# Scores of the last layer from high and low float32r halves instead of fp32 operands

## The chip, the cores and the metric

The kernel is one program on one core of a Trainium2 chip. The metric is device time in microseconds (us) of one execution, from launch to end. Three executions of the kernel before gave 3190.16, 3192.45 and 3198.47 us; their median, 3192.45 us, is what "before" means below. All durations inside the kernel come from one further execution that was profiled.

A core has a matrix engine (PE, with a separate row PEld for loading its stationary operand), three engines for elementwise work (DVE, ACT, POOL), and a queue, SP, which issues nearly all copies between DRAM and the on-chip memory here. A copy is moved by up to 16 DMA engines. Each engine runs its own instructions in order and waits for the others through semaphores. On-chip memory has 128 partitions; a matrix product contracts over partitions, and its result goes to PSUM, a separate memory that DVE and ACT read.

## The reference

The reference is a network of four layers on an input `x` of shape (4, 1024, 128). Each layer computes `x = x + s * silu(g)` with `s` from a mixing part and `g` from a feed-forward part, both on the normalized `x`. The change concerns the mixing part of the last layer, an attention with 16 heads of 8 numbers and a score that depends on distance:

```python
qx = split_head(x @ Wq.T)
kx = split_head(x @ Wk.T)
vx = split_head(x @ Wv.T)
ns = jnp.arange(n) + (MAXLEN - n)
ex = rel_embed[ns].reshape(n, NH, HD).transpose(1, 0, 2)
srel = srel_skew(jnp.einsum('bhnd,hmd->bhnm', qx, ex))
inv_dim = 1.0 / np.sqrt(d / NH)
qk = (jnp.einsum('bhnd,bhmd->bhnm', qx, kx) + srel) * inv_dim
mask = 1000000000.0 * jnp.triu(jnp.ones((n, n), dtype=x.dtype), 1)
atten = jax.nn.softmax(qk - mask, axis=-1)
out = jnp.einsum('bhnm,bhmd->bhnd', atten, vx).transpose(0, 2, 1, 3).reshape(b, n, d)
return out @ Wp.T + bp
```

`rel_embed`, the table of distance rows, has 256 rows while `n` is 1024, so most distances share one row; the kernel subtracts that row's vector from the others, and only a band of some four blocks of 128 columns beside the diagonal needs the distance term.

## The kernel before, in words

Layers 0 to 2 run first and end at about 2140 us of the profiled span. While layer 2 ends, `prepare3` (L1676) turns the weights of layer 3, and `begin_first` (L1864) makes the normalized input, the queries, the keys and the values of the first of the four batches and stores them in DRAM as `first["qk"]`, `first["vd"]` and `first["xnT"]`.

Layer 3 is `layer3` (L1725). Its work is cut into 16 groups: four batches, each with four sets `i` of four heads. A group has eight units, one for each block `t` of 128 query rows, taken in the order `ORDER3 = (7, 0, 6, 1, 5, 2, 4, 3)`, so that a long unit and a short one alternate. A unit with block `t` has (t+1) * 128 key columns, worked in tiles of at most 512; the units with t > 3 have two tiles, so a group has 12 tiles and the layer 192.

A head's 8 query numbers lie in partitions 32j to 32j+7 of a tile `q`, its keys in the same partitions of `k`, for j = 0 to 3; the other 24 of the 32 partitions of a head hold zeros, which `memset` (L1745) writes once. There are two pairs of `q` and `k`, used in turn by the groups. For each group:

- `project3` (L1968) loads `q` and `k` of the next group: four SP copies of 8 rows by 4096 bytes for `q`, and later four for `k` (L1975). The main loop asks for `q` at the first unit of a group (L1851) and for `k` at the third (L1854).
- `relative3` (L1992) multiplies 128 queries of two heads with the turned distance rows `W["emb"]` (L2004, tile `pr`), ACT copies the result to `r` (L2006), and SP stores `r` in a DRAM tile `flat` in four copies (L2009, L2010). It runs seven half-steps ahead of the unit that uses it.
- `shear3` (L2013) reads `flat` back with a row step one float short, which shifts every row by its distance (tile `rel`, L2025, L2027, L2031), and POOL masks and fills it with `select` (L2035). It runs three units ahead. The short units share one `rel` buffer, the long ones two.
- `scores3` (L2048) makes the scores: for one tile, four products, one a head, in the four 32-partition strips of PE (L2068, tile `score`, four times 512 floats of each partition of PSUM, one buffer). DVE adds `rel`, scales and keeps the minimum of the row (`neg`, L2076 and L2083, whose minimum is `low`), and ACT takes the exponent with a row sum (L2090).
- DVE transposes the weights in blocks of 32 (`wT`, L1797), and `weigh3` (L2096) multiplies them with the values on PE (L2104, tile `po`, 10240 instructions); `finish3` divides by the sums.

Beside a batch's groups run, in small steps, `ffn3` (L1942), the feed-forward part of that batch with its products `pgu` and `po` (L1953, L1963), and `begin3` (L1903), which makes queries, keys and values of the next batch and stores them as `seq["qk"]` (L1927). Most temporaries of these two, and `r`, take their place in turn from one pool of three buffers (tag `temp`).

The main loop (L1829 to L1859) writes out the order of all this for every engine. On PE, therefore, the scores of the next tile stand in one line with `pr`, `pgu` and both `po`. Every fp32 product is two instructions of PE and two weight loads in the profile: 192 tiles of four heads are 768 products of scores and 1536 instructions.

Of the kernel before, what the change touches and what calls it, by code (L numbers as in the profile page):

```python
# [10 lines left out]
F32 = mybir.dt.float32  # L11
BF16 = mybir.dt.bfloat16
I32 = mybir.dt.int32
AF = mybir.ActivationFunctionType
ALU = mybir.AluOpType
# [14 lines left out]
def _constants():  # L30
# [19 lines left out]
    parts.append(("sel16", (row // 16) == np.arange(8)[None, :]))  # L50

    parts.append(("rep8", np.where(row < 8, (col % 8) == row, 0.0)))

# [1613 lines left out]
def spread(a):  # L1667

    return a.rearrange("p (i j r) -> p i j r", j=4, r=32)[:, :, :, 0:8]
# [6 lines left out]
def prepare3(k, w, W, ps):  # L1676
# [20 lines left out]
    nc.gpsimd.tensor_copy(W["bpw"], W["bp"])  # L1697
    W["emb"] = new("emb", [P, 4, 256])
    with k.tc.tile_pool(name="pad3", bufs=1) as rp:
        pad = rp.tile([P, 2, 512], F32, tag="pad", name="pad")  # L1700
        nc.vector.memset(pad, 0.0)
        for c in range(2):
            for i in range(4):
                nc.gpsimd.tensor_copy(spread(pad[:, c, :])[:, i], heads_of(W["rel"][:, c, :])[:, i])
        for i in range(4):
            k.transpose_tiles(ps, "tr", [pad[:, c, i * P : (i + 1) * P] for c in (0, 1)], W["emb"][:, i, :])
            yield

        e0 = rp.tile([P, 4], F32, tag="e0", name="e0")
        nc.vector.tensor_copy(e0, W["emb"][:, :, 0])  # L1710
        for i in range(4):
            nc.vector.tensor_scalar(W["emb"][:, i, :], W["emb"][:, i, :], e0[:, i : i + 1], None, op0=ALU.subtract)
        nc.vector.tensor_scalar(W["emb"][:, :, 0], e0, -1.0, None, op0=ALU.mult)
# [11 lines left out]
def layer3(k, W, x3, out, eps5, ps, first):  # L1725
# [12 lines left out]
    with ExitStack() as st:  # L1738
# [123 lines left out]


def begin_first(k, W, pool, ps, x, eps5, first):  # L1864

# [8 lines left out]
    for n, name in enumerate(("WqT", "WkT")):  # L1874
        qk = pool.tile([P, T], F32, tag=("ret", "au")[n], name="qk")
        for half in range(2):
# [26 lines left out]
def begin3(k, W, p1, p2, temp, ps, dram, x3, b, eps5, seq):  # L1903
# [63 lines left out]

def project3(k, p2, pairs, seq, i, group):  # L1968

    nc = k.nc  # L1970
    q, kk = pairs
# [192 lines left out]
def tile_kernel(ctx: ExitStack, tc: tile.TileContext, I, out):  # L2164
# [11 lines left out]

    first = {name: store.tile(shape, F32, tag=name, name=name) for name, shape in (("qk", [2, P, T]), ("vd", [T, D]), ("xnT", [P, T]))}
    whole = ExitStack()
# [53 lines left out]
```

## Time and profile before

| What | Value |
|---|---|
| median of three executions | 3192.45 us |
| the profiled execution | 3191.88 us |
| its span from the first to the last instruction | 3190.2 us |
| layer 3 within the span | about 2144 to 3182 us |
| PE busy, whole span | 2246.5 us (70%) |
| DVE busy, whole span | 2302.6 us (72%) |
| ACT busy, whole span | 1494.7 us (47%) |
| POOL busy, whole span | 1155.6 us (36%) |
| mean granted clock of PE | 0.764 of full speed |
| score products, L2068 | 276.5 us in 1536 instructions |
| products with distance rows, L2004 | 227.5 us in 1024 instructions |

Busy time counts an instruction that executes; waiting, branching and the issuing of copies do not count. The instructions of PE are pipelined and overlap, so a mean duration is not the time between two starts. The number after a group's busy time in the profile is the mean of one instruction; behind the bar stands how long the engine sat idle just before that group's instructions and what ended the idle time. "issue" means that no releaser was found. The profile gives one line per group of instructions, by line of the kernel and by tile names `out<-in`.

### The profile page before, as it was taken

What the parts mean: (1) busy time and instruction counts of PE and PEld (TensorE: products, weight loads), DVE (VectorE), ACT (ScalarE), POOL (GpSimd) and SP (SyncE); (2) the same over time, 40 slices, a digit from 0 to 9 for tenths busy, and PEclk for the clock granted to TensorE, in tenths of its full rate; (3) what the DMA queues carried; (4) which work ended last, traced back from release to release, by engine and by line L of the source; (5) the groups of instructions that cost most, each with busy time, mean ns of one, the idle gap of its engine ahead of it and who ended that gap; (6) DMA issues with size and microseconds to landing.
All of it is one profiled execution on the core that took longest, in us unless ns stands there. A gap on an engine that the chain in (4) does not pass through costs nothing. (4 is left out here: it accounts for less than half of the span.)

```text
span 3190.2 us, 50621 instructions
## 1 busy us (share of the span) xinstructions
PE 2246.5 (70%) x18321; PEld 1278.9 (40%) x18321; DVE 2302.6 (72%) x5540; ACT 1494.7 (47%) x3256; POOL 1155.6 (36%) x1086
## 2 busy tenths in 40 slices
PE   5787778577787776894443674367877877878875
PEld 2555556232333332561110222244544544545553
DVE  5555544878888886657777888656788788788786
ACT  3554544333333333525332463136665765665663
POOL 3433444144444444223477433232322322323322
PEclk9888888588878877895655566566877877877776
DMA  3000000100000000320333446328677677677772
GB/s 81 13 1 1 1 1 1 35 0 0 0 0 7 6 1 7 114 98 20 73 106 112 128 107 145 101 90 252 179 217 213 191 215 230 185 221 203 209 233 65
DMA packets 397311, 308.18 MB, mean 97 GB/s; under 512 B 96369, under 2 KB 379885, under 8 KB 391429
## 3 DMA queue, kind: packets, MB, share of 16 engines
q1 hardware_dynamic: 395908, 300.75, 32.9%
q10 hardware_dynamic: 1152, 4.19, 0.4%
q8 instruction: 144, 2.36, 0.3%
q14 instruction: 107, 0.87, 0.1%
HBM read 162.72 MB, written 141.56 MB: 95 GB/s over the span
## 5 line engine op out<-in xcount | busy, mean ns | idle before, releaser
L2090 ACT ACTIVATE neg<-neg,low 128x640 f32<-128x640 f32 (+7 forms) x512 | 390.1, 763 | 168.4 <-DVE low L2083 168.1
L2035 POOL TENSOR_SCALAR_AFFINE_SELECT rel<-rel 128x512 f32<-128x512 f32 x288 | 180.2, 637 | 625.6 <-DMA rel<-flat 459.6
L1797 DVE STREAM_TRANSPOSE wT<-neg 128x640 f32<-128x640 f32 (+7 forms) x512 | 361.7, 754 | 15.8 <-ACT neg L2090 13.4
L2068 PE MATMUL score<-k,q 32*128 32x512 f32 (+3 forms) x1536 | 276.5, 702 | 103.1 <-DVE low L2083 102.5
L2083 DVE CUSTOM_DVE_ANT_0 neg<-score,rel,low 128x128 f32<-128x128 f32 (+3 forms) x448 | 217.3, 517 | 138.2 <-issue 67.2
L2004 PE MATMUL pr<-emb,q 32*128 32x256 f32 x1024 | 227.5, 525 | 62.2 <-ACT r L2006 37.1
L2104 PE MATMUL po<-wT,vb 128*32 128x64 f32 (+1 forms) x10240 | 216.6, 241 | 44.4 <-issue 30.8
L2104 PEld LDWEIGHTS po<-wT,vb 128*32 128x32 f32 x10240 | 184.3, 128 | 144.1 <-issue 85.2
L2004 PEld LDWEIGHTS pr<-emb,q 32*128 32x128 f32 x1024 | 146.1, 249 | 136.9 <-ACT r L2006 69.1
L2006 ACT COPY r<-pr 128x512 f32<-128x512 f32 x256 | 136.4, 581 | 128.8 <-PE pr L2004 95.3
L2068 PEld LDWEIGHTS score<-k,q 32*128 32x128 f32 x1536 | 98.5, 236 | 159.8 <-DVE low L2083 115.5
L2083 DVE CUSTOM_DVE_ANT_0 neg<-score,rel 128x512 f32<-128x512 f32 (+3 forms) x320 | 149.2, 521 | 18.4 <-PE score L2068 7.2
L835 PE MATMUL pg<-xnT,w 128*128 128x512 f32 x256 | 148.1, 662 | 6.7 <-DVE h L839 3.1
L788 POOL TENSOR_TENSOR prod<-rest,kv 128x2048 f32<-128x2048 f32 x32 | 145.2, 4571 | 18.4 <-ACT rest L778 18.4
L837 PE MATMUL pu<-xin,w 128*128 128x512 f32 x256 | 141.2, 635 | 13.7 <-DVE h L839 7.6
L826 PE MATMUL po<-h,w 128*128 128x512 f32 x256 | 131.4, 635 | 26.9 <-DVE h L839 26.9
L838 ACT ACTIVATE h<-pg 128x512 f32<-128x512 f32 x128 | 75.9, 595 | 156.8 <-PE pg L835 156.7
L214 PE MATMUL pt<-ident,three 128*24 128x128 bf16 x64 | 9.2, 295 | 197.5 <-DVE three L211 197.5
L1084 PE MATMUL ph<-xin,upT 128*128 128x512 bf16 (+1 forms) x128 | 69.7, 574 | 65.2 <-DVE xin L1078 63.8
L431 PE MATMUL px<-hT,xbcT 128*128 128x512 f32 x256 | 114.7, 592 | 0.0
L1489 PE MATMUL read<-kt,const_sb 128*128 128x128 f32 x256 | 50.7, 370 | 90.3 <-POOL kt L1484 90.3
L783 DVE TENSOR_REDUCE s<-prod 128x128 f32<-128x2048 f32 x32 | 73.1, 2284 | 49.4 <-POOL prod L788 49.4
(634 smaller groups left out, 5662.8 us busy)
## 6 DMA issues: line engine op xcount, KB each, us to landing
flat<-r SPq DMA_DIRECT2D x256, 256.0 KB
rel<-flat SPq DMA_DIRECT2D x112, 512.0 KB
flat<-r SPq DMA_DIRECT2D x256, 128.0 KB
rel<-flat SPq DMA_DIRECT2D x96, 256.0 KB
kt<-kd SPq DMA_DIRECT2D x16, 512.0 KB
qt<-qd SPq DMA_DIRECT2D x16, 512.0 KB
kdc<-kdd SPq DMA_DIRECT2D x16, 512.0 KB
ktc<-ktd SPq DMA_DIRECT2D x16, 512.0 KB
```

The lines of the kernel that those rows point to most:

```text
L788: nc.gpsimd.tensor_tensor(prod, attn.rearrange("p (t h g) -> p t h g", t=4, g=16)[:, t].unsqueeze(2).to_broadcast(each), kv[:, t, 1, :].re ...
L826: nc.tensor.matmul(po, W["w2"][:, e, c, :], h[:, c, :], start=(e == 0 and c == 0), stop=(e == 7 and c == 1))
L835: nc.tensor.matmul(pg, W["w1"][:, e, c * P : (c + 1) * P], xnT, start=True, stop=True)
L837: nc.tensor.matmul(pu, W["w3"][:, e, c * P : (c + 1) * P], xin, start=True, stop=True)
L1797: nc.vector.transpose(weights[at, pair][j][:, t % 2, 0 : (t + 1) * P], S[j][:, 0 : (t + 1) * P])
L2004: nc.tensor.matmul(to[:, m, :], q[at, t * P : (t + 1) * P], W["emb"][at, i, :], start=True, stop=True)
L2006: nc.scalar.copy(r[:, n], to)
L2035: nc.gpsimd.affine_select(out=rel[:, :, slot(back), :], in_=rel[:, :, slot(0), :], compare_op=op, fill=fill, base=0, pattern=[[0, 4], [-si ...
L2068: nc.tensor.matmul(sc[:, j, 0 : last - first], q[at(j), 1 + t * P : 1 + n], kk[at(j), first:last], start=True, stop=True)
L2083: nc.vector.tensor_tensor_reduce(out=neg[:, begin:last], in0=sc[:, j, begin - first : last - first], in1=rel[:, j, slot : slot + (last - b ...
L2090: nc.scalar.activation(neg[:, 0:n], neg[:, 0:n], AF.Exp, bias=here, scale=-1.0, accum_out=group["sums"][:, j, t : t + 1])
L2104: nc.tensor.matmul(o[32 * j : 32 * j + 32, 2 * pair + m.start : 2 * pair + 2, :], vb[:, kb, j].rearrange("p a d -> p (a d)"), weights[j][: ...
```

## The change

The queries, the keys and the distance rows are each written as the sum of a high part, the number rounded to the type float32r, and a low part, the rest. The 32 partitions of a head, of which 8 held numbers, now hold four rows of eight: `q` has high, high, low, low; `k` has high, low, high, low; and `W["emb"]` likewise, through the new column of constants `of_low`. Contracting over the 32 partitions gives the four products of high and low parts in one instruction of type float32r instead of one fp32 product.

The new function `halves3` makes the two parts: ACT rounds, SP stores the high part, POOL subtracts, SP stores the low part. It stands in `begin_first` (in two halves of 512 columns) and in the projections of `begin3`. The DRAM tiles `qk` have twice the size. `project3` loads 16 rows of 4096 bytes with each copy, and has eight copies for `q` and eight for `k` where it had four and four. The zeroing of `q` and `k` falls away but for one column. In `prepare3`, the distance rows are spread four times, and each of the four sets is rounded, subtracted, masked and added; the three matrices of the feed-forward part share one buffer `f`, in a pool of its own.

```diff
+    parts.append(("of_low", (row // 8 % 2 == 1) & (np.arange(1)[None, :] == 0)))
...
-    W["emb"] = new("emb", [P, 4, 256])
+    W["emb"] = w.tile([P, 4, 256], F32R, tag="emb", name="emb")
...
-        nc.vector.memset(pad, 0.0)
         for c in range(2):
-            for i in range(4):
-                nc.gpsimd.tensor_copy(spread(pad[:, c, :])[:, i], heads_of(W["rel"][:, c, :])[:, i])
+            for r in range(4):
+                nc.gpsimd.tensor_copy(
+                    pad[:, c, :].rearrange("p (n r d) -> p n r d", r=4, d=8)[:, :, r], W["rel"][:, c, :].rearrange("p (n d) -> p n d", d=8)
+                )
+        low = k.c("of_low")
+        top = rp.tile([P, 1], F32, tag="top", name="top")
+        nc.vector.tensor_scalar(top, low, -1.0, 1.0, op0=ALU.mult, op1=ALU.add)
         for i in range(4):
-            k.transpose_tiles(ps, "tr", [pad[:, c, i * P : (i + 1) * P] for c in (0, 1)], W["emb"][:, i, :])
+            emb = rp.tile([P, 256], F32, tag="emb", name="emb")
+            high = rp.tile([P, 256], F32R, tag="high", name="high")
+            e0 = rp.tile([P, 1], F32, tag="e0", name="e0")
+            k.transpose_tiles(ps, "tr", [pad[:, c, i * P : (i + 1) * P] for c in (0, 1)], emb)
+            nc.vector.tensor_copy(e0, emb[:, 0:1])
+            nc.vector.tensor_scalar(emb, emb, e0, None, op0=ALU.subtract)
+            nc.vector.tensor_scalar(emb[:, 0:1], e0, -1.0, None, op0=ALU.mult)
+            nc.scalar.copy(high, emb)
+            nc.vector.tensor_tensor(emb, emb, high.bitcast(F32), ALU.subtract)
+            nc.vector.tensor_scalar(emb, emb, low, None, op0=ALU.mult)
+            nc.vector.scalar_tensor_tensor(W["emb"][:, i, :], high.bitcast(F32), top, emb, op0=ALU.mult, op1=ALU.add)
             yield
...
+    with k.tc.tile_pool(name="f3", bufs=1) as rp:
         for name in ("gate", "up", "down"):
-            f = rp.tile([P, 3, D], F32, tag="f" + name, name="f" + name)
+            f = rp.tile([P, 3, D], F32, tag="f", name="f")
...
-            q, kk = p1.tile([P, 1 + T], F32, tag=f"q{n}", name="q"), p1.tile([P, T], F32, tag=f"k{n}", name="k")
-            for a in (q, kk):
-                (nc.gpsimd if n else nc.vector).memset(a, 0.0)
+            q, kk = p1.tile([P, 1 + T], F32R, tag=f"q{n}", name="q"), p1.tile([P, T], F32R, tag=f"k{n}", name="k")
+            nc.vector.memset(q[:, 0:1].bitcast(F32), 0.0)
...
+def halves3(k, high, a, to):
+
+    nc = k.nc
+    nc.scalar.copy(high, a)
+    nc.sync.dma_start(out=to[0], in_=high.bitcast(F32))
+    nc.gpsimd.tensor_tensor(a, a, high.bitcast(F32), ALU.subtract)
+    nc.sync.dma_start(out=to[1], in_=a)
...
-        nc.sync.dma_start(out=first["qk"][n], in_=qk)
+        for half, tag in enumerate(("a", "u")):
+            tok = slice(half * 512, (half + 1) * 512)
+            halves3(k, pool.tile([P, 512], F32R, tag=tag, name="high"), qk[:, tok], first["qk"][n, :, :, tok])
...
-    seq["qk"] = dram.tile([2, P, T], F32, tag="qk", name="qk")
+    seq["qk"] = dram.tile([2, 2, P, T], F32, tag="qk", name="qk")
...
-        nc.sync.dma_start(out=seq["qk"][n], in_=qk)
+        halves3(k, temp.tile([P, T], F32R, tag="temp", name="high"), qk, seq["qk"][n])
...
         for j in range(4):
-            nc.sync.dma_start(out=dst[32 * j : 32 * j + 8], in_=seq["qk"][n, 32 * i + 8 * j : 32 * i + 8 * j + 8])
+            rows = seq["qk"][n, :, 32 * i + 8 * j : 32 * i + 8 * j + 8]
+            part = dst[32 * j : 32 * j + 32].bitcast(F32)
+            for r in range(2):
+                if n == 0:
+                    nc.sync.dma_start(out=part[16 * r : 16 * r + 16], in_=rows[r].unsqueeze(0).to_broadcast([2, 8, T]))
+                else:
+                    nc.sync.dma_start(out=part[16 * r : 16 * r + 16], in_=rows)
         yield
```

More of the change, by code (lines that the diff above doesn't have):

```diff
@@ L13 @@
 I32 = mybir.dt.int32
+F32R = mybir.dt.float32r
 AF = mybir.ActivationFunctionType
@@ L1697, in prepare3 @@
     nc.gpsimd.tensor_copy(W["bpw"], W["bp"])
-    W["emb"] = new("emb", [P, 4, 256])
+    W["emb"] = w.tile([P, 4, 256], F32R, tag="emb", name="emb")
     with k.tc.tile_pool(name="pad3", bufs=1) as rp:
         pad = rp.tile([P, 2, 512], F32, tag="pad", name="pad")
-        nc.vector.memset(pad, 0.0)
         for c in range(2):
-            for i in range(4):
-                nc.gpsimd.tensor_copy(spread(pad[:, c, :])[:, i], heads_of(W["rel"][:, c, :])[:, i])
-        for i in range(4):
-            k.transpose_tiles(ps, "tr", [pad[:, c, i * P : (i + 1) * P] for c in (0, 1)], W["emb"][:, i, :])
-            yield
[L1709 to L1713, printed above, removed]
+            for r in range(4):
[5 more added lines that the diff above has]
+        nc.vector.tensor_scalar(top, low, -1.0, 1.0, op0=ALU.mult, op1=ALU.add)
+        for i in range(4):
+            emb = rp.tile([P, 256], F32, tag="emb", name="emb")
[9 more added lines that the diff above has]
+            nc.vector.scalar_tensor_tensor(W["emb"][:, i, :], high.bitcast(F32), top, emb, op0=ALU.mult, op1=ALU.add)
+            yield
@@ L1965, in ffn3, with project3 @@
             yield
-def project3(k, p2, pairs, seq, i, group):
+def project3(k, p2, pair, seq, i, group):
     nc = k.nc
-    q, kk = pairs
+    q, kk = pair
     group.update({"q": q, "k": kk, "sums": p2.tile([P, 4, NT], F32, tag="sums", name="sums")})
@@ L2175, in tile_kernel @@
     x3 = store.tile([P, NB * NT, D], F32, tag="x3", name="x3")
-    first = {name: store.tile(shape, F32, tag=name, name=name) for name, shape in (("qk", [2, P, T]), ("vd", [T, D]), ("xnT", [P, T]))}
+    first = {name: store.tile(shape, F32, tag=name, name=name) for name, shape in (("qk", [2, 2, P, T]), ("vd", [T, D]), ("xnT", [P, T]))}
     whole = ExitStack()
```

## The prediction

> **What bounds the kernel now.** I read the page's busy table and slices first. No engine is busy over 72% of the span, so the stage decides. The change lies in layer 3, from about 2144 us on, so the second view is the table by stage, cut at the start of the second group, inside, and at the end of the loads:
>
> ```profile
> core 0: us, PE busy (x) PEld busy (x) DVE busy (x) ACT busy (x) POOL busy (x), PEclk, DMA share, GB/s
> 2144.00:2176.00 32.00, 20.61 (x96) 13.76 (x96) 11.29 (x37) 14.58 (x27) 11.57 (x12) 0.55 0.95 274
> 2176.00:2616.00 440.00, 358.97 (x5594) 223.86 (x5590) 347.59 (x1104) 282.83 (x661) 126.35 (x178) 0.76 0.71 207
> 2616.00:3110.00 494.00, 401.31 (x6727) 255.92 (x6719) 399.05 (x1256) 310.82 (x736) 147.69 (x202) 0.78 0.73 213
> ```
>
> PE and DVE are both busy 81% of the steady stretch and take turns through the single `score` buffer; the DMA engines are busy 72% at the same time, more than anywhere before. The third view is DVE's waits from 2144 to 3110 us, since DVE would be the bound if PE were free:
>
> ```profile
> DVE neg L2083 <- issue: 73.0, 22, 8.0
> DVE neg L2083 <- PE score L2068: 50.8, 42, 3.9
> DVE neg L2076 <- PE score L2068: 31.7, 13, 12.7
> ...
> DVE neg L2083 <- POOL rel L2035: 8.8, 4, 3.8
> DVE neg L2083 <- PE pr L2004: 7.2, 3, 3.8
> ```
>
> The reader sees that DVE waits little for `rel`: the loads of `flat` arrive in time. What hides behind "issue" shows in the timeline of PE at the longest such wait, 7.97 us before 2778.97 us:
>
> ```profile
> 2772.26 0.59 PE L1953 MATMUL pgu<-xnT,upT 128*128 128x256 f32 x2
> 2773.86 0.49 PE L1963 MATMUL po<-downT,h 128*128 128x128 f32 x2 [1.01 <-POOL h L1959]
> 2774.54 0.49 PE L1963 MATMUL po<-downT,h 128*128 128x128 f32 x2 [0.19 <-POOL h L1959]
> 2774.96 0.70 PE L2068 MATMUL score<-k,q 32*128 32x256 f32 x4
> 2775.59 2.08 PE L1963 MATMUL po<-downT,h 128*128 128x128 f32 x8
> 2777.60 1.22 PE L2068 MATMUL score<-k,q 32*128 32x256 f32 x4
> ```
>
> The scores stand in PE's line behind `ffn3`, which the change leaves in fp32. The last view is the DMA table of the same window:
>
> ```profile
> q1 hardware_dynamic: 326670, 202.96, 72.1%
> ...
> qk<-qk SPq DMA_DIRECT2D x6, 512.0 KB
> q<-qk SPq DMA_DIRECT2D x64, 32.0 KB
> k<-qk SPq DMA_DIRECT2D x64, 32.0 KB
> ```
>
> **Products.** From the first start to the last end of its eight instructions, a 512-column tile of scores takes a median of 1.74 us (96 tiles), 384 columns 1.34 (32 tiles), 256 columns 0.86 (32), 128 columns 0.50 (32). The trace has no float32r. Its nearest single-pass rows are the bf16 products of 512 columns (L1084), 0.61 us each at half clock and 0.39 at full. Bounds: nothing gained, or a 512 tile at 0.39 to 0.61 us. I take 0.6, as the shape is the same, and 0.5, 0.4 and 0.35 for the short ones: 96 x 1.14 + 32 x (0.84 + 0.46 + 0.15) = 156 us of PE freed. `pr` (227.5 us busy) has half its instructions and a single pass; at a third, 150 us are freed. On the path is only what DVE waits for: 50.8 + 31.7 + 7.2 = 90 us, less 12.7 us in which the pipe first fills. The 73 us of "issue" stay, being `ffn3`. Of the 77 us left I take 55, since `po` and `pgu` still stand ahead of the scores; bounds 0 and 77. ACT's wait for `pr` (95.3 us) feeds `flat` early and is off the path.
>
> The clock: the table grants 0.76 to 0.78 where PE is busy 81% and 0.55 where it is 64%. With 306 us fewer of 824, PE is near 50%, so I expect some 0.55 to 0.65, which is why the half-clock durations were used above. The Trainium skill (TensorE: Matmul & The Clock Gate, Part 1) says that the gate knows only full and half speed and falls back after an idle window of about 3.4 us; by it alone, layer 3 would run at half clock wherever PE pauses that long, and the remaining fp32 products would take up to twice as long. That would eat most of the 55 us, not turn it over.
>
> **Loads of q and k.** This is the part that I hold decisive. Eight copies per group become sixteen, each of 16 rows of 4096 bytes: 256 packets a group instead of 64. In the packet records, a 4096-byte packet took 159 ns in a steady row of them and 212 ns on average near the loads of `q` and `k`. Spread over 16 engines, 192 more packets cost 192 x 0.16 to 0.21 / 16 = 1.9 to 2.5 us a group, which 72% leaves room for. But the records of semaphores show how a copy is spread: the 24-row load of `pick` gets 12 separate increments, the 4-row load of `wdt` 4, each 8-row load of `q` 8 (the rest in one step at issue), and copies of 32 or 128 rows 16. So a copy runs on as many engines as evenly divide its outermost length. The new sources are two sets of eight rows; their outermost length is 2, so I expect two engines, eight packets on each.
>
> The Trainium skill (DMA: Bandwidth & Descriptors, section "Why a DMA increments its semaphore by 16 and not by 1") states this: k is the largest number up to 16 that divides both patterns' slowest dimension, and copies issued by SP take the lowest-numbered k engines. The trace agrees with the count (12, 4, 8); no row names the engine. By the page all sixteen copies of a group fall on the same two.
>
> Without the engines' names I bound it: at best other pairs each time, so 1.9 to 2.5 us as above; at worst the same two, with 16 x 8 = 128 packets, 128 x 0.159 to 0.212 = 20.4 to 27.1 us a group on each. I take the upper end of this sharing with the cheap packet, because two copies issued in one row are nearest to the steady row. The other traffic is 72.1% of the 62.5 us that a group takes (the first `q` copies of groups 1 and 15 are issued at 2172.6 and 3048.0 us; 875.4 / 14), less 0.8 for the old loads: 44 us. Saturated stretches of 4 us show packet times summing to about 1.08 of 16 engines. So the two engines need (44 + 20.4) / 1.08 = 60 us a group, or 66 with the dear packets. With PE's gain a group would want to take 62.5 - 55/15 = 59 us. The two engines thus have work for the whole group, and every `flat` and `rel` copy, which needs all 16, queues behind them. A burst of eight copies holds them for 10 us; the load of `rel` now lands a median of 13 us before DVE uses it (4 at the least after the first group), and the short units' single buffer keeps it from being asked for earlier. SP's copies use eight semaphores in turn, and an issue waits for the copy before it on the same one, so SP itself stalls next: behind the waiting copies stand `flat` stores, and behind them `rel` loads, for which POOL and then DVE wait.
>
> PE too: the first `pr` of the next group starts 4 to 18 us after `q` is asked for (median 14) and stands ahead of scores. Eight copies on two engines land after 10 us plus the 3 to 5 of today plus what is queued; in half of the groups PE will wait some 3 to 8 us.
>
> Together I take a group at 65 us: the 60 that the two engines need, with 8% of idle time from the dependences. Bounds 59 (hidden) and 71 (66 with the same idle). 15 groups x (65 - 62.5) = +38 us; this replaces the gain of 55.
>
> **The small parts.** `halves3` in `begin3`, six times: an ACT copy of 128x1024 (about 1.14 us, L2090's 128x1024 form), a POOL operation (2.34 us, L228) and a second 512 KB store. POOL is busy 30% here and hides it; two of the three `temp` buffers are held up to 6.5 us longer, for which ACT's copies to `r` wait. These run seven half-steps ahead: +4 us, bounds 0 and 39. In `begin_first`, four POOL operations of 128x512 (1.27 us) stand among the last POOL steps of layer 2: +3, bounds 0 and 8. `W["emb"]` gains 16 DVE operations net of 0.35 us and four ACT copies, in a stretch where DVE has gaps, and `f` in one buffer makes three short steps follow one another: +2, bounds 0 and 8. The memsets take 0.9 us on each of DVE and POOL side by side: -1. SP issues eight more copies a group at about 0.4 us: hidden while SP waits for `rel` buffers (207 us for DVE).
>
> **Sum** against the profiled execution, 3191.88 us (span 3190.2, 0.6 below the median): +38 + 4 + 3 + 2 - 1 = +46, so 3238 us.
>
> **Rivals.** (1) The forecast: two engines carry the loads and set the pace, 3190 to 3340 us; 0.60. (2) The loads are hidden, by more engines, by rotating pairs, or by the slack of 13 us; then DVE sets the pace and the products' gain comes through: 3192 - 55 + 8 = 3145, between 3115 (77 gained) and 3185. For it: DVE hardly waits for `rel` today. Against it: the counted increments. It decides if the pair of engines needs under 58 us a group. 0.28. (3) The loads are spread, but `q` lands late and PE stands: 15 x 5 us against the 55 gained, 3192 + 75 - 55 + 8 = 3220; 0.07. For it: 4 us of slack in some groups. (4) float32r in four strips is no faster, or gain and loss cancel: 3192 to 3215; 0.05.
>
> **Numbers.** Likeliest 3238; its own range 3195 to 3320. The range 3115 to 3320 leaves out 1 in 10 at either end. 0.3% (10 us) is about what a measurement of this kernel can tell from no change. Faster: most of (2) and the low edge of (1), 0.30. Same: the edges of (1), (2) and (4), 0.07. Slower: 0.63.
>
> **What would show it.** Scores: 768 instructions and a 512 tile of about 0.6 us, granted clock lower. Loads: two separate increments per copy, landing 10 us or more after issue, DVE waits for `rel` growing from 9 us to over 60, PE waits for `q` growing from 10. The forecast is wrong if a copy shows 8 or 16 increments, or if groups take under 61 us.

## The result and the profile after

The changed kernel takes 3376.66 us (median, 3375.09 to 3379.82) where the kernel before took 3191.41 beside it: a ratio of 1.0577, 95% interval 1.0559 to 1.0595. That is a loss of 185 us; the forecast was a loss of 46, and its range ended at 3320. The profiled execution has a span of 3373.0 us.

In short, from the runs below: the cheaper product gains about 61 us, the new loads of `q` and `k` lose 125, the split itself loses 10, and 85 are lost because the whole last layer is issued in another order. 26 us stay open. From here on TensorE is the engine PE, VectorE is DVE, ScalarE is ACT and GpSimd is POOL. A ratio is a kernel's time over that of the kernel before, run beside it, with its 95% interval in brackets.

The table by stage of the changed kernel, cut at the same times as the prediction's:

```profile
core 0: us, PE busy (x) PEld busy (x) DVE busy (x) ACT busy (x) POOL busy (x), PEclk, DMA share, GB/s
2144.00:2176.00 32.00, 8.18 (x24) 5.12 (x24) 0.66 (x4) 4.39 (x8) 7.65 (x5) 0.50 0.40 123
2176.00:2616.00 440.00, 250.33 (x4250) 175.53 (x4249) 296.21 (x925) 255.38 (x573) 113.09 (x154) 0.66 0.65 192
2616.00:3110.00 494.00, 277.60 (x5152) 190.36 (x5154) 346.49 (x1085) 269.07 (x619) 129.75 (x166) 0.65 0.65 191
```

TensorE (PE) is busy 57% of the steady stretch instead of 81%, as it should be with one instruction where there were two. But VectorE (DVE) did not move up into the room: it fell from 80% to 69%, and the DMA engines from 72% to 65%. Every engine is less busy than before. A group takes 74.8 us, counted from the first `q` copy of group 1 to that of group 15 (1047.4 / 14); it was 62.5. Fourteen groups give 14 x 12.3 = 172 us. The first `q` copy of group 1 is already issued 19 us later (2191.9 us instead of 2172.6), and about 8 us are won back after the last load: together 183 us, as the two spans differ. The late start is the first fill, where the first subtraction with `rel` starts at 2183.2 us instead of 2162.4.

DVE's waits in the changed kernel, from 2144 to 3110 us (engine, line, what it waited for, us in total, times, longest):

```profile
DVE neg L2110 <- POOL rel L2062: 107.7, 34, 11.9
DVE neg L2103 <- PE score L2095: 60.4, 17, 24.7
DVE neg L2110 <- issue: 37.7, 33, 3.2
DVE wT L1807 <- ACT neg L2117: 30.9, 27, 4.1
DVE neg L2110 <- POOL h L1980: 25.7, 3, 9.0
DVE neg L2110 <- DMA rel<-flat: 18.2, 2, 9.1
```

The wait for scores shrank by 15 us (82.5 to 67.7, of which 7.3 are at L2110 and not shown), and 24.7 us of what is left is the first fill (12.7 before). "Issue" fell by half. What is new is `rel`: 108 us for POOL's selects and 18 for the loads themselves, where POOL's were 9 before.

The DMA view of the last stretch, and SP's issue of one `q` copy (shortest, median and longest ns), in the changed kernel:

```profile
q1 hardware_dynamic: 141752, 93.63, 64.0%
...
q<-qk SPq DMA_DIRECT2D x56, 64.0 KB
k<-qk SPq DMA_DIRECT2D x48, 64.0 KB
```

```profile
L2000 SPq DMA_DIRECT2D q<-qk x104: 591/592/632, 2191.9 to 3085.2; - x104
```

The same line of the kernel before:

```profile
L1975 SPq DMA_DIRECT2D q<-qk x56: 263/293/815, 2225.7 to 3057.7; - x56
```

An issue takes twice as long, and there are twice as many. In the semaphore records each new copy has one step at issue and then exactly two separate increments, so it ran on two engines as foreseen. A group's eight `q` copies have all landed 12.9 to 16.5 us after the first was issued; the four of the kernel before took 4 to 6 us in most groups and 11 to 12.5 in every fourth.

### The profile page after: what moved, and what is told of

The parts are those of the page before. It is cut to its first block, busy times and chain, and to the rows that moved or that the text cites. A ratio compares the mean times of both kernels' runs of the same rounds, so it can differ in the third digit from the quotient of the medians.

```text
span 3373.0 us, 48274 instructions
## 1 busy us (share of the span) xinstructions
PE 2094.6 (62%) x17041; PEld 1229.3 (36%) x17041; DVE 2321.3 (69%) x5558; ACT 1526.5 (45%) x3284; POOL 1166.6 (35%) x1094
## 5 line engine op out<-in xcount | busy, mean ns | idle before, releaser
L1807 DVE STREAM_TRANSPOSE wT<-neg 128x640 f32<-128x640 f32 (+7 forms) x512 | 376.4, 764 | 58.7 <-ACT neg L2117 39.4
L2095 PE MATMUL score<-k,q 32*128 32x512 f32 (+3 forms) x768 | 137.1, 605 | 327.0 <-DVE low L2110 314.6
L2110 DVE CUSTOM_DVE_ANT_0 neg<-score,rel,low 128x128 f32<-128x128 f32 (+3 forms) x448 | 215.8, 514 | 147.4 <-issue 35.5
L2131 PE MATMUL po<-wT,vb 128*32 128x64 f32 (+1 forms) x10240 | 258.8, 255 | 75.1 <-DVE wT L1807 56.3
L2131 PEld LDWEIGHTS po<-wT,vb 128*32 128x32 f32 x10240 | 210.7, 136 | 133.9 <-DVE wT L1807 83.3
L2110 DVE CUSTOM_DVE_ANT_0 neg<-score,rel 128x512 f32<-128x512 f32 (+3 forms) x320 | 149.8, 522 | 104.2 <-POOL rel L2062 93.8
L2031 PE MATMUL pr<-emb,q 32*128 32x256 f32 x512 | 133.8, 424 | 112.5 <-ACT r L2033 59.7
L2095 PEld LDWEIGHTS score<-k,q 32*128 32x128 f32 x768 | 62.6, 253 | 386.9 <-DVE low L2110 302.4
L839 PE MATMUL pu<-xin,w 128*128 128x512 f32 x256 | 140.5, 632 | 12.9 <-DVE h L841 7.4
L2031 PEld LDWEIGHTS pr<-emb,q 32*128 32x128 f32 x512 | 91.5, 260 | 152.5 <-ACT r L2033 77.3
L2103 DVE TENSOR_SCALAR_CACHE_REDUCE neg<-score 128x384 f32<-128x384 f32 (+2 forms) x192 | 79.7, 415 | 68.0 <-PE score L2095 68.0
L2016 POOL COPY vb<-vr 32x1024 f32<-32x1024 f32 x64 | 66.2, 1034 | 146.7 <-PE po L2131 99.1
```

Of the source, the lines that this page charges most:

```text
L839: nc.tensor.matmul(pu, W["w3"][:, e, c * P : (c + 1) * P], xin, start=True, stop=True)
L1807: nc.vector.transpose(weights[at, pair][j][:, t % 2, 0 : (t + 1) * P], S[j][:, 0 : (t + 1) * P])
L2031: nc.tensor.matmul(to[:, m, :], q[at, t * P : (t + 1) * P], W["emb"][at, i, :], start=True, stop=True)
L2095: nc.tensor.matmul(sc[:, j, 0 : last - first], q[at(j), 1 + t * P : 1 + n], kk[at(j), first:last], start=True, stop=True)
L2110: nc.vector.tensor_tensor_reduce(out=neg[:, begin:last], in0=sc[:, j, begin - first : last - first], in1=rel[:, j, slot : slot + (last - b ...
L2131: nc.tensor.matmul(o[32 * j : 32 * j + 32, 2 * pair + m.start : 2 * pair + 2, :], vb[:, kb, j].rearrange("p a d -> p (a d)"), weights[j][: ...
```

## What stands in the prediction and was wrong from the start

The section on the kernel says that the main loop writes out the order of the work for every engine, and the prediction takes that order as fixed. It is not. The loop writes the program; the framework's scheduler then orders each engine's instructions anew. The comparison of two instruction lists shows it. In the pair "wide" and "wide_fp32" below, the source differs in nothing but the operand type of two lines. Of TensorE's 10188 instructions only 5367 stand at the same place in both programs, of SP's 1213 only 413. So changing a product's type also changes when everything in the last layer is issued. From "before_r" on the order is therefore held where it has to be.

A smaller misreading: by the prediction's own rows DVE is busy 80% of the steady stretch, not 81%. Nothing hangs on it.

## Experiments: loads and products, each with its own order

**wide.** The loads alone are mended: a group's `q` and `k` come in one 128-row copy each.

```diff
-    nc.sync.dma_start(out=to[0], in_=high.bitcast(F32))
+    for r in ((0, 1), (0, 2))[n]:
+        nc.sync.dma_start(out=to[:, r], in_=high.bitcast(F32))
...
-    nc.sync.dma_start(out=to[1], in_=a)
+    for r in ((2, 3), (1, 3))[n]:
+        nc.sync.dma_start(out=to[:, r], in_=a)
...
-    seq["qk"] = dram.tile([2, 2, P, T], F32, tag="qk", name="qk")
+    seq["qk"] = dram.tile([2, 16, 4, 8, T], F32, tag="qk", name="qk")
...
-        for j in range(4):
...
+        nc.sync.dma_start(out=dst.bitcast(F32), in_=seq["qk"][n, 4 * i : 4 * i + 4].rearrange("j r d t -> (j r d) t"))
```

> The changed kernel, but the DRAM tile qk holds each head's 32 rows side by side, so that a group's q is loaded by one copy of 128 rows and its k by another; to make this, each half is stored twice (four stores of 512 KB where there were two). If the two engines that carry the narrow copies are the cause of the loss (theory A), the group's period falls from 74.8 us to 59 to 62 us and the time to 3120 to 3185 us. If the float32r products themselves or the lower clock are the cause (theory B), the period stays above 70 us and the time above 3300 us. If the cause is the halving work and its stores in begin3 (theory C), the groups that hold begin3 (every fourth) stay near 80 us, and the time is 3230 to 3300 us.

Measured: 3239.74 us, ratio 1.0135 (1.0110 to 1.0160). A group takes 66.9 us. Most of the loss goes with the narrow loads, but the gain of the products does not come through. The time lies in the range of theory C, the halving work; `split_small` below puts that work at about 10 us, so theory C is not the reason.

**wide_fp32** and **narrow_fp32.** The same split and the same loads (wide ones, and the change's own), with both products in fp32 again:

```diff
-            nc.tensor.matmul(to[:, m, :], q[at, t * P : (t + 1) * P], W["emb"][at, i, :], start=True, stop=True)
+            nc.tensor.matmul(to[:, m, :], q[at, t * P : (t + 1) * P].bitcast(F32), W["emb"][at, i, :].bitcast(F32), start=True, stop=True)
...
-                sc[:, j, 0 : last - first], q[at(j), 1 + t * P : 1 + n], kk[at(j), first:last], start=True, stop=True
+                sc[:, j, 0 : last - first], q[at(j), 1 + t * P : 1 + n].bitcast(F32), kk[at(j), first:last].bitcast(F32), start=True, stop=True
```

> As wide, but both products read the same tiles as fp32, with two instructions again. Theory A: the difference to wide is the worth of the float32r product alone, 40 to 70 us, so this kernel is at 3185 to 3215 us. Theory B: it is faster than wide.

> The changed kernel with its narrow copies, both products reading the same tiles as fp32. Theory A: as slow as the changed kernel or slower, 3370 to 3450 us. Theory B: close to the kernel before, under 3250 us.

Measured: wide_fp32 3222.55 us, 1.0077 (1.0051 to 1.0103); narrow_fp32 3335.11 us, 1.0435 (1.0411 to 1.0458). With either kind of load the cheaper product makes the kernel slower, by 17 and 42 us. wide_fp32 is faster than wide, as theory B had it; narrow_fp32 lies between the ranges of both theories. Either float32r costs something that no row shows, or the order that comes with it does.

**act_queue.** The change's own copies, issued by ScalarE instead of SP:

```diff
-                    nc.sync.dma_start(out=part[16 * r : 16 * r + 16], in_=rows)
+                    nc.scalar.dma_start(out=part[16 * r : 16 * r + 16], in_=rows)
```

(the same for the other of the two copies)

> The changed kernel, but the sixteen narrow copies of a group are issued by ACT instead of SP; they still run on two engines. If the loss comes from SP's line and its semaphores, which stand still behind the narrow copies (theory A1), the time falls to 3150 to 3250 us. If it comes from the two engines themselves, behind which every flat and rel copy queues (theory A2), it stays above 3300 us.

Measured: 3415.91 us, 1.0686 (1.0661 to 1.0711), slower still. Taking 16 issues a group off SP does not help when ScalarE has to make them. It does not say that SP's time is free, since ScalarE is itself on the way to `rel`, and the order was planned anew here too.

## Experiments: the product with the order held

In before_r and the three runs with "order" in their names, the program is planned with one operand type, and the operand type of the 1280 instructions is replaced afterwards, so that every instruction of every engine keeps its place:

```diff
     with tile.TileContext(nc) as tc:
         tile_kernel(tc, I, out)
+    retype(nc, F32R)
```

**before_r** does that to the kernel before, with nothing split.

> The kernel before with every instruction of every engine in its old place; only the operand type of the 768 score products and the 512 relative products is float32r (one pass instead of two). Nothing is split: queries, keys and distance rows go in with fewer bits, so the output is coarser. 'The product is cheaper, and the loss comes from the order that the planner chose': the vector engine's 90 us of waiting for scores shrink as the prediction had it, 3141 us (3120 to 3175). 'The product itself costs time' (a lower granted clock takes back what a pass saves): 3197 to 3235. Half of each: about 3170.

Measured: 3134.33 us, 0.9810 (0.9793 to 0.9827), a gain of 59 to 61 us where the prediction had put 55 on the path. Its DVE waits, 2144 to 3050 us:

```profile
DVE neg L2084 <- issue: 53.5, 22, 8.2
DVE neg L2084 <- PE score L2069: 25.4, 31, 3.5
DVE neg L2077 <- PE score L2069: 23.5, 8, 7.9
DVE wT L1798 <- ACT neg L2091: 18.9, 24, 2.4
DVE neg L2084 <- POOL rel L2036: 10.4, 4, 8.4
```

Beside the lines of the kernel before: scores 82 to 49 us, "issue" 73 to 54, and `rel` at 10 instead of 9. TensorE was granted less clock here (0.70 and 0.71 in the rows):

```profile
2176.00:2616.00 440.00, 294.36 (x5480) 204.44 (x5484) 371.58 (x1185) 301.95 (x708) 134.94 (x190) 0.70 0.76 222
2616.00:3050.00 434.00, 284.85 (x5555) 200.21 (x5548) 370.68 (x1165) 288.41 (x683) 138.60 (x189) 0.71 0.78 224
```

That is 0.70 instead of 0.77, and the whole gain came in spite of it. The Trainium skill (TensorE: Matmul & The Clock Gate, Part 1) was cited in the prediction for a gate that could eat most of the 55 us; this run doesn't agree with that use of it, and no run here shows which idle windows moved the clock.

**wide_order32** and **wide_orderR**: the two orders of the wide pair, exchanged.

> The kernel with 16-engine loads, in which every engine's order is the one planned for fp32 products (that of the kernel that took 3222.6 us), and the products are float32r all the same. Planner theory (the same instructions in another order lost the gain): under 3222.6 by 20 to 60 us, 3165 to 3200. Clock theory (float32r costs by itself): 3240, as the float32r kernel with its own order (3239.7).

> The mirror: 16-engine loads, the order planned for float32r products (3239.7 us with them), and fp32 products in it. Planner theory: the order is the bad part, and two passes make it worse yet, 3260 to 3310. Clock theory: 3222, as the fp32 kernel with its own order.

Measured: wide_order32 3181.67 us, 0.9962 (0.9949 to 0.9974); wide_orderR 3397.45 us, 1.0640 (1.0616 to 1.0664). With the two orders as rows of one table (us):

| 16-engine loads | fp32 products | float32r products |
|---|---|---|
| order planned for fp32 | 3222.6 | 3181.7 |
| order planned for float32r | 3397.5 | 3239.7 |

Along each row float32r gains (41 and 158 us); down each column the float32r order loses (175 and 58 us). The apparent loss of 17 us is the diagonal. wide_orderR lies far above the 3260 to 3310 that was expected for it: fp32 products suffer more from that order than was thought. DVE's waits from 2160 to 3100 us, in wide and then in wide_order32, the same instructions in two orders:

```profile
DVE neg L2105 <- POOL rel L2057: 80.6, 21, 8.2
DVE neg L2105 <- issue: 54.2, 26, 7.7
DVE neg L2098 <- PE score L2090: 23.7, 7, 5.0
DVE neg L2105 <- PE score L2090: 19.7, 16, 2.7
DVE neg L2105 <- POOL h L1982: 17.2, 6, 4.9
```

```profile
DVE neg L2105 <- PE score L2090: 67.7, 44, 11.3
DVE neg L2105 <- issue: 33.6, 17, 8.3
DVE wT L1807 <- ACT neg L2112: 29.6, 29, 5.1
DVE neg L2105 <- POOL rel L2057: 11.4, 5, 7.7
```

In the float32r order scores come earlier (43 us of waiting at both lines instead of 77, of which 9 are not shown). It pays for that with `rel`, 81 us instead of 11: the chain product, copy, store, sheared load, select is late for it. Where in the chain the lateness begins, these lines do not tell. wide_order32 is also a kernel with the split that is a little faster than the one before.

**narrow_order32**: the change's own loads, planned for fp32, with float32r in it.

> The changed kernel (two-engine loads) with the order planned for fp32 products (3335.1 us with fp32 products) and float32r products in it. Planner theory: 3290 to 3335, that is 40 to 85 us under the changed kernel, at equal products and equal loads. Clock theory: 3375.

Measured: 3305.88 us, 1.0353 (1.0333 to 1.0373), 71 us less than the change at equal products and copies. Nothing differs but the order, on all engines.

**pin_pool** and **pin_pe**: planned for float32r, but one engine is tied to its order of the fp32 plan by edges that fix the order and wait for nothing:

```diff
+        todo = [n for n in names[e] if n in here and here[n].engine == e]
+        for before, after in zip(todo, todo[1:]):
+            tc.add_manual_dep(here[after], before, info, reason="pin")
```

> 16-engine loads, float32r products, planned for float32r (3239.7 us), except that GpSimd alone is held to its order of the fp32 plan (with all engines in that order: 3181.7). 'GpSimd's place of the value copies is the cost' (there GpSimd waits 175 us of the stretch for TensorE before it may copy vb, 67 in the fp32 order, and the selects behind it make VectorE wait 81 us against 11): 3182 to 3200. 'TensorE's order is the cost' (relative products and ffn products put later): 3230 to 3245. Both: between.

> The same with TensorE alone held to its order of the fp32 plan, GpSimd planned for float32r. 'TensorE's order': 3182 to 3200. 'GpSimd's order': 3225 to 3245.

Measured: pin_pool 3210.45 us, 1.0051 (1.0035 to 1.0066), half of the 58 us; pin_pe 3186.22 us, 0.9984 (0.9971 to 0.9996), nearly all. "GpSimd's place of the value copies" had a good line in its favour. In the float32r order POOL waits long before it copies `vb` (2160 to 3100 us, wide, then wide_order32):

```profile
POOL vb L2011 <- PE po L2126: 175.0, 13, 21.7
```

```profile
POOL vb L2011 <- PE po L2126: 67.3, 14, 7.6
```

But it is the smaller cause or a part of the larger one: with TensorE's order alone put back, POOL free, the time is nearly all won back. DVE's wait for `rel` does not tell the two apart: it falls to 21 us in pin_pe and to 29 in pin_pool. What differs on TensorE, by the two lists: between wide_fp32 and wide the 96 down-projection products of `ffn3` are moved back by 57 places on average and the 512 `pr` products by 8 (single ones by up to 170, of some 420 a group). Between the kernel before and the changed one it is 33 and 27 places. Between narrow_order32 and the changed kernel, 71 us apart, the down-projection moves forward by 8 and `pr` back by 17, so a late down-projection is not needed for the loss. Which of the moves costs the time was not tried.

A rival stands beside TensorE's moves. A pinned engine leaves the others to be planned anew, and ScalarE's order changes with TensorE's. In the last layer ScalarE changes between the exponent (L2112) and the silu of `ffn3` (L1980, L1987), and the profile shows a table load of 1.283 us where it does. ScalarE's table loads for two of these lines (2144 to 3200 us, wide, then wide_order32):

```profile
L2112 ACT ACT_TABLE_LOAD x32 | 41.1, 1283 | 0.6
L1987 ACT ACT_TABLE_LOAD x16 | 20.5, 1283 | 0.3
```

```profile
L2112 ACT ACT_TABLE_LOAD x17 | 21.8, 1283 | 0.3
L1987 ACT ACT_TABLE_LOAD x3 | 3.8, 1283 | 0.1
```

The whole layer has 63 of them in wide, 45 in pin_pool, 31 in pin_pe and 33 in wide_order32, in step with the times but for the last two, which are 5 us apart; the 30 more of wide are 38 us of ScalarE, which also copies `r` for `rel`. So the 58 us may be in part table loads; no run holds ScalarE's order alone. They are not the whole of the order's price: the changed kernel and narrow_order32 both have 47.

## Experiments: the loads with the order held

**sixteen16** and **sixteen2** have the same instructions at the same place on every engine. Both load a group by 16 copies of 16 rows; in the second, a gap of one row between a copy's two halves keeps them from being one run of rows:

```diff
-                nc.sync.dma_start(out=dst[at : at + 16].bitcast(F32), in_=rows[2 * r : 2 * r + 2].rearrange("r d t -> (r d) t"))
+                nc.sync.dma_start(out=dst[at : at + 16].bitcast(F32), in_=rows[2 * r : 2 * r + 2, 0:8])
...
-    seq["qk"] = dram.tile([2, 16, 4, 8, T], F32, tag="qk", name="qk")
+    seq["qk"] = dram.tile([2, 16, 4, 9, T], F32, tag="qk", name="qk")
```

> Order planned for fp32 products, float32r in it, queries and keys of a group loaded by 16 copies of 16 rows as in the changed kernel, but from rows that lie one after the other, so that each copy is spread over 16 DMA engines. 'The two engines of a copy cost the time': 3180 to 3215, near the kernel with two 128-row copies (3181.7). 'The number of copies and SP's time to issue them costs it' (16 x 0.6 us a group): 3290 to 3310, as narrow_order32 (3305.9).

> The same instructions in the same order on every engine as the run before; the only difference is a gap of one row in DRAM between the two halves of a copy's rows, so that a copy is split over two engines as in the changed kernel. 'Two engines': 3290 to 3310. 'Number of copies': the same as the run before to within 10 us.

Measured: sixteen16 3256.83 us, 1.0199 (1.0175 to 1.0223); sixteen2 3324.02 us, 1.0409 (1.0389 to 1.0428). Both theories had a part. Two engines instead of sixteen cost 67 us, with a group's `q` landing 13.3 to 16.0 us after its first issue (5.8 to 9.5 in sixteen16). Some of SP's waits show one way in which this reaches the rest (2144 to 3110 us, sixteen16, then sixteen2; L2051 loads `rel`, L2035 and L2036 store `flat`):

```profile
SPq L2051 <- DVE low L2109: 62.4, 32, 5.6
```

```profile
SPq L2051 <- DVE low L2109: 28.4, 17, 3.6
SPq L2036 <- DMA q<-qk: 27.7, 32, 2.4
SPq L2035 <- DMA q<-qk: 24.4, 29, 1.5
```

In sixteen2 SP waits 109 us in all behind copies of `q` and `k`, mostly before it may store `flat`; in sixteen16 not at all. The other runs in which SP issues two-engine copies have 80 to 118 us of it (105 in the changed kernel), the kernel before 0.5. That is what the prediction said would come next: an issue waits for the copy before it on the same semaphore. But 16 copies over 16 engines are still 75 us over two wide ones, and here the order differs again.

**sixteen16_pin_pe** and **after_pin_pe** take that apart: TensorE's products in the order planned for fp32 and two wide loads, the other engines planned around it. The second is the changed kernel itself, each of its instructions kept.

> 16 copies a group, each over 16 engines, float32r, TensorE's matmuls in the order planned for fp32 products and two wide loads. 'The 75 us between sixteen16 and wide_order32 are order': 3182 to 3200. 'They are the price of issuing 16 copies': 3245 to 3260.

> The changed kernel with all its own instructions and its two-engine loads; only TensorE's matmuls are held to the order planned for fp32 products and two wide loads a group, the other engines planned anew around it. If TensorE's order is the whole of what float32r lost (71 us against narrow_order32) and also of what 16 copies cost beside two (75 us, sixteen16 against wide_order32), what stays is the two engines' 67 us: 3250. If the 16 copies themselves cost those 75 us: 3300 to 3315. If the order does not matter here: 3377.

Measured: sixteen16_pin_pe 3233.79 us, 1.0121 (1.0094 to 1.0148); after_pin_pe 3293.71 us, 1.0311 (1.0284 to 1.0337). Both lie between their theories, nearer to "the copies themselves cost it". DVE's waits in sixteen16_pin_pe and in after_pin_pe, 2160 to 3100 us:

```profile
DVE neg L2111 <- POOL rel L2063: 75.6, 18, 11.2
DVE neg L2111 <- issue: 58.8, 48, 4.2
DVE neg L2111 <- PE score L2096: 26.5, 11, 7.0
```

```profile
DVE neg L2114 <- POOL rel L2066: 100.3, 31, 11.6
DVE neg L2114 <- issue: 85.1, 37, 11.3
DVE neg L2107 <- PE score L2099: 37.9, 15, 24.9
```

With 16 copies, `rel` is late even when every copy is spread and TensorE's order is the good one; two engines add to it. SP takes 0.30 to 1.83 us for each of the spread copies, median 0.42:

```profile
L2003 SPq DMA_DIRECT2D q<-qk x120: 302/418/1825, 2179.3 to 3100.7; - x120
```

Sixteen of them are 6.7 us a group of SP's line, and the `flat` stores and `rel` loads stand in the same line. That this is how the 51 us of the table below come about fits the lines; SP's line by itself was not varied with the order held. pin_pe is the nearer neighbour of sixteen16_pin_pe, since there too only TensorE is held; against it the price is 44 us (0.9984 to 1.0121).

## Experiments: what the split itself costs

**split_small** and **loads_small** start from wide_order32 and hold every engine's order. The first leaves the split out (its two operations run on one column), the second also loads only a quarter of each row.

```diff
-    nc.scalar.copy(high, a)
+    w = 1 if SMALL else a.shape[-1]
+    nc.scalar.copy(high[:, 0:w], a[:, 0:w])
...
+        w = 256 if SMALL else T
+        nc.sync.dma_start(out=dst[:, 0:w].bitcast(F32), in_=seq["qk"][n, 4 * i : 4 * i + 4].rearrange("j r d t -> (j r d) t")[:, 0:w])
```

> wide_order32 (3181.7 us) with every engine held to that order, and the split of the queries and keys left out: ScalarE's copy and GpSimd's subtraction run on one column instead of 512 or 1024, and the unsplit rows are stored in all four places, so that every load and store moves the same bytes and the scores are of other numbers. 'The split's work makes up the 47 us against before_r (3134.3)': 3134 to 3150. 'The four-fold bytes and stores do': 3172 to 3185.

> The run before (the split left out, every engine held to the same order, 3174.4 us), and the two wide loads of a group bring only a quarter of each row, 256 KB a group instead of 1 MB, as much as the kernel before loads; what they leave is zeros written once. 'The four-fold bytes of the loads hold up the other transfers, and make up the 40 us that are left against before_r (3134.3)': 3134 to 3150. 'They do not; it is the order and the tiles that are loaded as a whole': 3166 to 3176.

Measured: split_small 3174.36 us, 0.9931 (0.9908 to 0.9953); loads_small 3165.00 us, 0.9890 (0.9866 to 0.9913). The work of the split is worth about 10 us, the four-fold bytes of the loads about 13. Neither is the bulk of the distance to before_r (3134.3).

## Where the 185 us are

By the ratios, since the runs stand beside different runs of the kernel before, times 3192 us; half a 95% interval from the two intervals in each step:

| step | ratios | us |
|---|---|---|
| products in one pass, every instruction in its place | 1 to 0.9810 | -61 ± 5 |
| not taken apart further | 0.9810 to 0.9890 | +26 ± 9 |
| four-fold bytes of the loads | 0.9890 to 0.9931 | +13 ± 10 |
| the split's two operations | 0.9931 to 0.9962 | +10 ± 8 |
| 16 copies a group instead of two wide ones | 0.9962 to 1.0121 | +51 ± 10 |
| two engines a copy instead of sixteen | 1.0121 to 1.0311 | +61 ± 12 |
| TensorE's order as planned for the change, and what the other engines' plans make of it | 1.0311 to 1.0577 | +85 ± 10 |
| sum | 1 to 1.0577 | +184 |

A chain of steps always adds up to the whole, so the sum confirms nothing; each step stands on its own pair of runs. The steps are not independent: TensorE's order costs 48 us with wide loads (0.9984 to 1.0135) and 85 with the change's. The kernel before has 8 spread copies a group, between the 2 and the 16 of the fifth step. The 26 us hold whatever else differs between before_r and loads_small: two loads that wait for a whole tile instead of eight, four stores instead of one, the preparation of the distance rows, and the order. They stay open. The sixth step has two stores a split instead of four in it; the pair sixteen16 and sixteen2, with nothing but the engines in it, gives 67.

## Why the prediction was wrong, step by step

Beside the table above, the forecast was: products -55, loads +93 (its 38 replaced the gain of 55), small parts +8, order nothing. Measured were -61, +125 (51, 61 and 13), +10 and +85, and 26 us stay open.

- **Products.** The term on the path was right: 55 us forecast, 59 to 61 measured. Its parts were rougher. A 512-column tile takes 0.80 us (median of 92, 4 instructions in before_r), not 0.6, against 1.56 in the kernel before counted the same way (tiles that other work interrupts for over 0.3 us left out; the prediction's 1.74 has them in). The relative products freed 112 us up to 3100 us, not 150:

In the kernel before, then in before_r (2144 to 3100 us; the instruction count, busy us, mean ns, idle before; the profile prints f32 for float32r too):

```profile
L2004 PE MATMUL pr<-emb,q 32*128 32x256 f32 x1016 | 226.3, 525 | 62.2 <-ACT r L2006 37.1 <-DMA q<-qk 10.3 <-ACT g L1964 6.8
L2068 PE MATMUL score<-k,q 32*128 32x512 f32 x712 | 160.7, 869 | 50.7 <-DVE low L2083 50.7
```

```profile
L2005 PE MATMUL pr<-emb,q 32*128 32x256 f32 x512 | 114.0, 436 | 104.0 <-ACT r L2007 61.3 <-DMA k<-qk 15.0 <-ACT g L1965 11.9
L2069 PE MATMUL score<-k,q 32*128 32x512 f32 x380 | 70.9, 681 | 78.4 <-DVE low L2084 78.1
```

  Some of the "issue" that was to stay behind `ffn3` went too (73.0 to 53.5 us, in a view that ends 60 us earlier as the kernel does). The clock fell to 0.70 here and to 0.65 in the changed kernel, where 0.55 to 0.65 was expected.
- **The order**, the first failed step. It is no term of the sum at all: the sum adds costs to instructions that stay where they are. It is worth 85 us with TensorE's order exchanged and 71 with all engines' (narrow_order32), the largest single item; without it the result would lie at about 3292, inside the range. Which moves cost it stays open. The trace of before could not give its price, but it could have told that there was one to look for: VectorE's order in the trace is not that of the program (at 3126.96 us a transpose stands between two subtractions, L2076 and L2083, that the program writes one behind the other).
- **Loads of q and k.** Two engines, landing over 10 us after issue, DVE's wait for `rel` from 9 to over 60, PE's wait for `q` before `pr` from 10.3 to 41.8 us: all as forecast. The Trainium skill's rule (DMA: Bandwidth & Descriptors, "Why a DMA increments its semaphore by 16 and not by 1") agrees with the two increments of every copy. The price was taken from the wrong picture. The forecast let the two engines run out of throughput. An estimate by its own formula with what was measured, (0.65 x 74.8 - 256 x 0.159 / 16 + 20.4) / 1.08, gives 62 us of work in a group of 74.8, so by it they are not full; no row shows the load of a single engine. What the rows show is the second half of its argument: SP stands 105 us behind the copies of `q` and `k`, and DVE then waits for `rel`. This costs 61 us by this step and 67 in the pair with nothing else changed. That the 93 us of the whole term are not far from 125 is partly luck, since SP's issues were not in them.
- **SP's issues**, the second failed step: "eight more copies a group at about 0.4 us: hidden". They take 0.59 us each as built. With spread copies, 16 instead of two cost 44 to 51 us. The hiding was argued from SP's waits for `rel` buffers, 207 us. That reserve did not last. The largest such wait in the kernel before and in the changed one, 2144 to 3110 us:

```profile
SPq L2025 <- DVE low L2083: 175.6, 65, 7.3
```

```profile
SPq L2052 <- DVE low L2110: 10.2, 7, 1.7
```

  With both lines that load `rel`, SP waits 200 us for the buffers in wide_order32, 76 in sixteen16_pin_pe and 12 in the changed kernel: there the buffers are mostly free when SP comes to them.
- **The first fill** was not costed: DVE's wait for the first scores grew by 12.0 us, a wait of 11.9 us for the first `rel` stands behind it, and the first subtraction with `rel` comes 20.8 us later than before. It is part of the two engines' price: sixteen2 issues the first `q` copy of group 1 at 2191.3 us, sixteen16 at 2176.5. DVE's timeline in the changed kernel:

```profile
2170.78 0.56 DVE L2103 TENSOR_SCALAR_CACHE_REDUCE neg<-score 128x384 f32<-128x384 f32 x1 [24.65 <-PE score L2095]
...
2183.20 0.35 DVE L2110 CUSTOM_DVE_ANT_0 neg<-score,rel,low 128x128 f32<-128x128 f32 x1 [11.86 <-POOL rel L2062]
```

- **The small parts.** The copy and the subtraction of `halves3`, in `begin3` and `begin_first` together, measured 10 ± 8 where +4 and +3 were forecast, right within the bounds; the further stores are in the open 26. The bytes, "72% leaves room for", cost 13 ± 10.
- **The rivals.** The second (loads hidden, 3145) describes before_r at 3134: it was right on the product and wrong on the loads. The first named the right suspect but only a third of the loss. No rival had the order in it.

## What to carry to other kernels

Find out first who orders the instructions: where a scheduler does, as here, a cheaper instruction can move half of the others, and a change is priced fairly only with the order held; a good old order may be worth keeping by hand. Count a copy by the number of engines it is spread over and by its place in the issuing queue, not by its bytes; sixteen small copies in the queue of the critical chain are not free even where that queue waits a lot. When a change makes every engine less busy at once, look for lateness in the chain, not for a full resource.

## What was not expected of the hardware

- SP's issue time depends on the form of the copy: 0.29 us (8 rows, median), 0.42 (16 rows in one run), 0.59 (two sets of 8 rows).
- A 512-column tile of scores, four products on 32 rows each, took 0.80 us in float32r against 1.56 in fp32; for 128 columns there is nearly no difference (0.48 and 0.50).
- In three kernels the granted clock of the stage was lower where TensorE was less busy (0.77 at 81%, 0.70 at 66%, 0.65 at 57%), and the stage with 0.70 was nevertheless faster by its full forecast.
- A table load of ScalarE took 1.283 us, and the planned order set how many there were in the layer: 63 in wide, 33 in wide_order32.
- Where SP issues two-engine copies, it waited behind copies of `q` and `k` for 80 to 118 us of the layer; with copies over sixteen engines, for 0 to 3.
